# Graph attention on one core: Wh of six graphs computed later from x kept on chip, theta of four graphs spread by TensorE, a fixed order in the first stages

## The chip, the core and the metric

The kernel runs on one core of a Trainium2 chip. TensorE (PE) multiplies, VectorE (DVE) and ScalarE (ACT) work element by element, GpSimd (POOL) does small steps and issues DMAs, SyncE (SP) only issues DMAs. Each engine takes its instructions in order; data pass between engines by semaphores. The metric is the device time of one launch in microseconds (us), the median of several runs.

## What is computed

Two graph-attention layers over 16 graphs (B) of 1024 nodes (N) and 256 features (F). Only layer 0 is touched by the change:

```
Wh  = einsum('bnf,of->bno', h, W)        # h is x
ei, ej = Wh @ a1, Wh @ a2
att = ei[:, :, None] + ej[:, None, :]
att = bn(att, g1, b1)                    # statistics over batch and rows
att = where(att >= 0, att, 0.2 * att)
att = bn(att, g2, b2)
att = softmax(att, axis=2) * adj
h'  = elu(bn(einsum('bij,bjo->bio', att, Wh), g3, b3))
x   = layernorm(x + h')
```

Layer 1 is an attention with four heads over the same adjacency; it takes two more products of x with vectors made from W, w1 and w2 (eight columns, "xw").

## The kernel before

Nodes are tiled as K = 8 blocks of P = 128, features as C = 2 blocks. Layer 0 runs in three stages, each with its own pools of SBUF and PSUM.

**Stage A (lines 224 to 311).** `vectors1` loads W of layer 1 (W1s) and makes the eight extra columns WW on DVE (16 wprod steps). WX holds the transposed W0 (256 columns), W0 times a1 and a2 (2) and WW (8): FX = 266 columns. For each graph, x is loaded (six buffers), two node blocks at a time (kk) are transposed by PE into PSUM (L285), copied by ACT to xT (L291), multiplied with WX by PE (L295) and copied by DVE to wx (L299, three buffers). Columns 0 to 255 go to DRAM (wh_dram, L300), two columns to eT (L301), eight to DRAM (xw_dram, L302). `parameters1` (L196) loads layer 1's small parameters at graph 1 and adds 1 to bias1 at once. `shifted1` (L191) reloads W1s moved by one row; it is called in the attention stage. `casts.behind` makes POOL wait for a datum and then issues a DMA that converts one graph's adjacency from f32 to bf16; it is called at four graphs of stage A, once in the statistics and at every third graph of stage B. `mask` (L139) loads a converted adjacency transposed.

**Stage B (lines 324 to 518).** First the statistics of the first normalisation, a chain of some 40 small DVE steps with two PE column sums (L332) and one POOL power (L148), which ends in ec, c1 and theta. theta and ec are turned to rows by PE (`to_rows`, L341), copied by ACT and stored to DRAM. Then, for each graph, th = theta spread over 128 partitions comes back from DRAM (L435; four buffers, four loads on ACT's queue, the others on SP's), and eight comparisons of th with ec (five on DVE, L440; three on ACT, L444) are multiplied by PE with the powers of ec (L451, 64 products of 7 columns). The sums give the second normalisation's mean and variance (`moments`).

**Attention stage (lines 523 to 653).** `weights` makes e and em for one node block (two ACT and three DVE steps of 128x1024), `aggregate` multiplies em with Wh (L578), `divisors` makes 1/sum (L555, L565), `store` divides (L593) and stores. For one graph the loop runs all k of the first half of the rows, then all k of the second.

Layer 1 (from 821 us on in the profile) follows an order written out by hand (`tc.manual_schedule`). The stages before it are ordered by the scheduler of the language, which places each engine's instructions by its own priorities; calls marked `keep_in_program_order` keep their place.

Of the kernel before, what the change touches and what calls it, by code (L numbers as in the profile page):

```python
# [8 lines left out]
F32 = mybir.dt.float32  # L9
BF16 = mybir.dt.bfloat16  # L10
# [9 lines left out]
P = 128  # L20
# [7 lines left out]
def kernel(  # L28
# [129 lines left out]
    xw_dram = [dpool.tile([N, 2 * H], F32, name=f"xw_dram_{b}") for b in range(B)]  # L158
# [5 lines left out]
    def vectors1(wp, wps):  # L164


        for fc in range(C):
            nc.sync.dma_start(
                W1s[:, fc], W[:, fc * P : (fc + 1) * P, :].rearrange("h p o -> p h o")
            )  # L170
        wbc = wp.tile([P, 2, H, F], F32, name="wbc")
        nc.sync.dma_start(wbc[:, 0], w1.partition_broadcast(P))
        nc.sync.dma_start(wbc[:, 1], w2.partition_broadcast(P))
        for fc in range(C):
            for s in range(2):
                for h in range(H):
                    prod = wp.tile([P, F], F32, tag="prod", name=f"wprod_{fc}_{s}_{h}", bufs=2)
                    nc.vector.tensor_tensor_reduce(
                        out=prod, in0=W1s[:, fc, h, :], in1=wbc[:, s, h, :], scale=1.0, scalar=0.0,
                        op0=ALU.mult, op1=ALU.add, accum_out=WW[:, fc, s * H + h : s * H + h + 1],  # L180
                    )
        pc = wps.tile([P, 2 * H], F32, tag="aps", name="pc")
# [13 lines left out]
    def parameters1():  # L196
        nc.sync.dma_start(bias1, bias.partition_broadcast(P))
        nc.vector.tensor_scalar(bias1, bias1, 1.0, None, ALU.add)
        nc.sync.dma_start(fb_bc[:, 0:H], lb1.partition_broadcast(P))
        nc.sync.dma_start(fb_bc[:, H : 2 * H], lb2.partition_broadcast(P))  # L200
        nc.sync.dma_start(al_bc, alpha.partition_broadcast(P))
        nc.vector.tensor_scalar(om_bc, al_bc, -1.0, 1.0, ALU.mult, ALU.add)
# [3 lines left out]
    with ExitStack() as l0:  # L206
# [17 lines left out]
        with tc.tile_pool(name="apool", bufs=1) as apool, tc.tile_pool(  # L224
            name="aps", bufs=2, space=PSUM
        ) as aps, tc.tile_pool(name="aps_w", bufs=4, space=PSUM) as aps_w:
            vectors1(apool, aps)
            xin = {}

            def load_x(b):  # L230
                xin[b] = apool.tile([P, K, F], F32, tag="x", name=f"x0_{b}", bufs=6)
                nc.sync.dma_start(xin[b], x[b].rearrange("(k p) f -> p k f", p=P))

            rows = apool.tile([P, P], F32, name="rows")
            nc.vector.memset(rows, 0.0)
            w0 = apool.tile([P, C, F], F32, name="w0")
            nc.scalar.dma_start(w0, W0.rearrange("(c p) f -> p c f", p=P))
            at = 0
            col = {}
            for name, v in (  # L240
                ("a1", a1), ("a2", a2), ("g1", g1), ("b1", b1),
                ("g2", g2), ("b2", b2), ("g3", g3), ("b3", b3),
            ):
                n = v.shape[0] // P
                nc.scalar.dma_start(rows[at : at + n, :], v.rearrange("(k p) -> k p", p=P))
                col[name] = (at, at + n)
                at += n
            for b in range(min(6, B)):
                load_x(b)
            pv = aps.tile([P, P], F32, tag="aps", name="pv")  # L250
            nc.tensor.transpose(pv, rows, ident)
            nc.vector.tensor_copy(vecs, pv)

            def vec(name):
                lo, hi = col[name]
                return vecs[:, lo:hi]

            WX = apool.tile([P, C, FX], F32, name="WX")
            nc.vector.tensor_copy(WX[:, :, F2:FX], WW)
            for fc in range(C):  # L260
                pt = aps.tile([P, F], F32, tag="aps", name=f"pw_{fc}")
                for oc in range(C):
                    nc.tensor.transpose(
                        pt[:, oc * P : (oc + 1) * P], w0[:, oc, fc * P : (fc + 1) * P], ident
                    )
                nc.vector.tensor_copy(WX[:, fc, 0:F], pt)
                pa = aps.tile([P, 2], F32, tag="aps", name=f"pa_{fc}")
                for oc in range(C):
                    nc.tensor.matmul(
                        pa,  # L270
                        w0[:, oc, fc * P : (fc + 1) * P],
                        vecs[:, oc : oc + C + 1 : C],
                        start=(oc == 0),
                        stop=(oc == C - 1),
                    )
                nc.vector.tensor_copy(WX[:, fc, F:F2], pa)

            KK = 2
            for b in range(B):
                wx = apool.tile([P, K, FX], F32, tag="wx", name=f"wx_{b}", bufs=3)  # L280
                for kk in range(K // KK):
                    px = aps.tile([P, KK, C, P], F32, tag="px", name=f"px0_{b}_{kk}")
                    for k in range(KK):
                        for fc in range(C):
                            nc.tensor.transpose(  # L285
                                px[:, k, fc, :],
                                xin[b][:, kk * KK + k, fc * P : (fc + 1) * P],
                                ident,
                            )
                    xT = apool.tile([P, KK, C, P], F32, tag="xT", name=f"xT0_{b}_{kk}", bufs=3)  # L290
                    nc.scalar.copy(xT, px)  # L291
                    for k in range(KK):
                        pw = aps_w.tile([P, FX], F32, tag="w", name=f"pw0_{b}_{kk}_{k}")
                        for fc in range(C):
                            nc.tensor.matmul(  # L295
                                pw, xT[:, k, fc, :], WX[:, fc, :],
                                start=(fc == 0), stop=(fc == C - 1),
                            )
                        nc.vector.tensor_copy(wx[:, kk * KK + k, :], pw)  # L299
                nc.sync.dma_start(wh_dram[b], wx[:, :, 0:F])  # L300
                nc.vector.tensor_copy(eT[:, b], wx[:, :, F:F2])  # L301
                nc.sync.dma_start(xw_dram[b].rearrange("(k p) w -> p k w", p=P), wx[:, :, F2:FX])  # L302
                if b % 3 == 1 and b < 12:
                    casts.behind(eT[0:1, b, 0, 0:1])
                if b + 6 < B:
                    load_x(b + 6)
                if b == 1:
                    parameters1()
            while casts.b < 2:
                casts.behind(eT[0:1, B - 1, 0, 0:1])  # L310
            mts = {b: mask(mpool, b, "mt0") for b in range(min(2, B))}

        epool = l0.enter_context(tc.tile_pool(name="epool", bufs=1))
        wh, ebs = {}, {}
# [8 lines left out]

        with tc.tile_pool(name="bpool", bufs=1) as bpool, tc.tile_pool(
            name="bps", bufs=2, space=PSUM
        ) as bps, tc.tile_pool(name="bps_t", bufs=2, space=PSUM) as bps_t:


# [12 lines left out]
            def to_rows(dst, src, nm):  # L341
# [6 lines left out]

            ei = small(qpool, "ei", [B, K])
            nc.vector.tensor_copy(ei, eT[:, :, :, 0])  # L350
            g_mean = column_sums("g_mean", ei)
            e_mean = small(qpool, "e_mean", [1])
# [4 lines left out]
            nc.vector.tensor_scalar(ec, ei, e_mean, None, ALU.subtract)  # L357
            dev_i = small(qpool, "dev_i", [B, K])
            nc.vector.tensor_tensor(
                dev_i, ei, g_mean.unsqueeze(2).to_broadcast([P, B, K]), ALU.subtract  # L360
            )
            nc.vector.tensor_tensor(dev_i, dev_i, dev_i, ALU.mult)
            g_var = column_sums("g_var", dev_i)
            v_mean = small(qpool, "v_mean", [1])
            nc.vector.tensor_reduce(v_mean, g_var, AX.X, ALU.add)
            nc.vector.tensor_scalar(v_mean, v_mean, 1.0 / B, None, ALU.mult)
            ejT = small(qpool, "ejT", [K, B])
            nc.vector.tensor_copy(ejT, eT[:, :, :, 1].rearrange("p b k -> p k b"))
            f_mean = small(qpool, "f_mean", [K])
            nc.vector.tensor_reduce(f_mean, ejT, AX.X, ALU.add)  # L370
            nc.vector.tensor_scalar(f_mean, f_mean, 1.0 / B, None, ALU.mult)
# [8 lines left out]
            nc.vector.tensor_tensor(dev, dev, dev, ALU.mult)  # L380
            var1 = small(qpool, "var1", [K])
            nc.vector.tensor_reduce(var1, dev, AX.X, ALU.add)
            nc.vector.tensor_scalar(var1, var1, 1.0 / B, v_mean, ALU.mult, ALU.add)
            tmp1 = small(qpool, "tmp1", [K])
            inv_std(s1, var1, tmp1)
            nc.vector.tensor_tensor(s1, s1, vec("g1"), ALU.mult)
            s1_b = s1.unsqueeze(2).to_broadcast([P, K, B])
            nc.vector.tensor_tensor(q, q, s1_b, ALU.mult)
            nc.vector.tensor_tensor(
                c1, q, vec("b1").unsqueeze(2).to_broadcast([P, K, B]), ALU.add  # L390
            )

            casts.behind(c1[0:1, 0, 0:1])
            sgn = small(qpool, "sgn", [K])
# [31 lines left out]
            for b in range(B):  # L431
# [24 lines left out]
                if b % 3 == 1:  # L456
                    casts.behind(sums[0:1, 0, 0, b : b + 1])
# [1437 lines left out]
```

## Time and profile before

| | us |
|---|---|
| Timed runs, median of 3 | 2285.81 (2285.52 to 2290.79) |
| The profiled execution's own time | 2298.42 |
| Its span in the trace | 2296.6 |
| PE busy | 2026.6 |
| DVE busy | 1833.9 |
| ACT busy | 1441.7 |
| POOL busy | 938.0 |
| Layer 0, up to the last store's statistics | 821 |

The profile comes from one execution. Busy time is the time in which an engine has an instruction running; matmuls overlap, so a busy PE is not a PE at its peak. "PEclk" or "granted clock" is the TensorE clock that the throttle granted, 1.00 being full speed. A wait is given as the engine and line that waited, the engine and line that ended the wait, the total, the number of times and the longest. SPq and POOLq are DMA issues. A product with f32 operands appears as two passes on PE, so stage A's 256 products are 512 rows.

### The profile page before, as it was taken

How to read it: one execution, taken by the hardware profiler on the slowest of the kernel's cores; microseconds unless marked ns; L12 is line 12 of the kernel's file. 1: busy time of each engine (PE TensorE's matmuls, PEld its weight loads, DVE VectorE, ACT ScalarE, POOL GpSimd, SP SyncE). 2: the span in 40 equal slices, each digit the busy share in tenths (PEclk: the TensorE clock that was granted, in tenths of full speed). 3: DMA queues.
4: the chain of work that ended last, by engine and by line, in shares of the span. 5: the costliest groups of instructions: out<-in, count | busy, mean ns of one | idle time of the engine just before them, and what ended most of it. 6: DMA issues, size and time to landing. Idle time of an engine off the chain costs nothing. (4 is left out here: it accounts for less than half of the span.)

```text
span 2296.6 us, 35722 instructions
## 1 busy us (share of the span) xinstructions
PE 2026.6 (88%) x12023; PEld 1578.7 (69%) x12023; DVE 1833.9 (80%) x4480; ACT 1441.7 (63%) x3156; POOL 938.0 (41%) x1005
## 2 busy tenths in 40 slices
PE   6785368999999955999999999999999999999995
PEld 5574334444444434888788888888888888888885
DVE  3234699999999855889889889789889789789784
ACT  1111677777777523686776776767767767767674
POOL 0000000000000005666666667657667667667671
PEclk9998568999999976999999999999999999999998
DMA  8797969997566126765766666756756756756650
GB/s 243 194 268 179 284 151 202 223 225 193 157 164 165 73 96 192 201 178 172 179 178 173 191 172 171 194 155 167 206 158 166 215 154 168 204 163 173 138 142 21
DMA packets 344669, 404.68 MB, mean 176 GB/s; under 512 B 189929, under 2 KB 291357, under 8 KB 334237
## 3 DMA queue, kind: packets, MB, share of 16 engines
q1 hardware_dynamic: 293533, 258.40, 40.1%
q0 software_dynamic: 49728, 141.39, 25.6%
q10 hardware_dynamic: 1216, 2.51, 0.3%
q8 instruction: 98, 1.61, 0.3%
q14 instruction: 94, 0.77, 0.1%
HBM read 330.90 MB, written 104.88 MB: 190 GB/s over the span
## 5 line engine op out<-in xcount | busy, mean ns | idle before, releaser
L1338 POOL DMA_INDIRECT xc<-xe_dram,ix x640 | 687.3, 1074 | 209.1 <-issue 181.3
L1657 PE MATMUL pv<-W1s,sT 128*128 128x256 f32 x2048 | 503.5, 390 | 0.4 <-ACT sT L1651 0.4
L578 PE MATMUL pa<-em,wh 128*128 128x512 f32 x1024 | 452.0, 599 | 17.7 <-DVE em L542 13.4
L1657 PEld LDWEIGHTS pv<-W1s,sT 128*128 128x128 f32 x2048 | 380.5, 196 | 43.8 <-ACT sT L1651 0.8
L1634 PEld LDWEIGHTS pt<-MX,s 125*128 125x128 f32 x2560 | 350.6, 204 | 30.7 <-ACT sT L1644 9.8
L578 PEld LDWEIGHTS pa<-em,wh 128*128 128x128 f32 x1024 | 193.7, 192 | 251.0 <-issue 235.6
L1634 PE MATMUL pt<-MX,s 125*128 125x100 f32 x2560 | 351.4, 286 | 5.4 <-ACT sT L1644 3.0
L1562 PE MATMUL pu<-xc,w 128*125 128x256 f32 x1280 | 347.1, 391 | 1.3 <-ACT s L1628 1.2
L1628 ACT ACTIVATE s<-pu,z 125x256 f32<-125x256 f32 x640 | 261.5, 474 | 82.8 <-DVE z L1620 57.4
L1671 ACT ACTIVATE m<-v,neg 128x512 f32<-128x512 f32 x256 | 183.7, 718 | 200.2 <-DVE v L1665 142.7
L1562 PEld LDWEIGHTS pu<-xc,w 128*125 128x125 f32 x1280 | 232.6, 192 | 36.5 <-issue 5.7
L1644 ACT COPY sT<-pt 128x500 f32<-128x500 f32 x256 | 144.2, 563 | 110.9 <-PE pt L1634 110.9
L534 ACT ACTIVATE e<-eb,c,s 128x1024 f32<-128x1024 f32 x128 | 155.0, 1236 | 79.0 <-DVE sm L548 42.7
L1714 POOL TENSOR_TENSOR ors<-ors,mhalf 128x1 f32<-128x1 f32 x128 | 110.8, 865 | 202.1 <-DVE ors L1708 200.7
L1665 DVE TENSOR_TENSOR v<-pv,x 128x512 f32<-128x512 f32 x256 | 174.9, 683 | 10.9 <-PE pv L1657 10.5
L538 ACT ACTIVATE e<-e,v,u 128x1024 f32<-128x1024 f32 x128 | 152.3, 1229 | 22.7 <-DVE e L537 16.6
L542 DVE TENSOR_TENSOR em<-e,mt 128x1024 f32<-128x1024 f32 x128 | 155.7, 1218 | 3.4 <-PE pa L578 2.1
L295 PE MATMUL pw<-WX,xT 128*128 128x266 f32 x512 | 130.3, 409 | 27.8 <-DVE wx L299 12.3
L537 DVE SCALAR_TENSOR_TENSOR e<-e 128x1024 f32<-128x1024 f32 x128 | 151.5, 1217 | 0.0
L299 DVE COPY wx<-pw 128x266 f32<-128x266 f32 x128 | 55.0, 434 | 115.6 <-PE pw L295 98.5
L1435 PE MATMUL pz<-IW,h 128*128 128x136 f32 x512 | 90.2, 308 | 56.7 <-DVE fs L1452 33.1
L291 ACT COPY xT<-px 128x512 f32<-128x512 f32 x64 | 34.5, 588 | 165.9 <-PE px L285 165.9
(301 smaller groups left out, 3148.3 us busy)
## 6 DMA issues: line engine op xcount, KB each, us to landing
x<-in_x_dram SPq DMA_DIRECT2D x32, 1024.0 KB
adj<-in_adj_dram POOLq DMA_DIRECT2D x16, 2048.0 KB
rw<-adj SPq DMA_DIRECT2D x32, 1024.0 KB
A<-u_dram SPq DMA_DIRECT2D x128, 250.0 KB
xe_dram<-x SPq DMA_DIRECT2D x16, 1060.0 KB
wh_dram<-wx SPq DMA_DIRECT2D x16, 1024.0 KB
wh<-wh_dram SPq DMA_DIRECT2D x16, 1024.0 KB
h_dram<-hb SPq DMA_DIRECT2D x16, 1024.0 KB
```

The costliest lines, as they stand in the source:

```text
L534: nc.scalar.activation(e, ebs[b], AF.Identity, bias=c1[:, k, b : b + 1], scale=s1[:, k : k + 1])
L537: nc.vector.scalar_tensor_tensor(e, e, SLOPE, e, ALU.mult, ALU.max)
L538: nc.scalar.activation(e, e, AF.Exp, bias=v2[:, k : k + 1], scale=u2[:, k : k + 1])
L542: nc.vector.tensor_tensor(em, e, mts[b][:, k, :], ALU.mult)
L578: nc.tensor.matmul(acc[b, hf, oc].rearrange("p k q -> p q k"), wh[b][:, k, oc * P : (oc + 1) * P], ems[b, k][:, hf * HALF : (hf + 1) * HAL ...
L1338: nc.gpsimd.indirect_dma_start(out=self.xc[:, i, :], out_offset=None, in_=xe_dram[g.b % 2], in_offset=bass.IndirectOffsetOnAxis(ap=g.l.ix[ ...
L1562: nc.tensor.matmul(pu[0:QR, 0:F], c.w[:, k].rearrange("p h q -> p (h q)"), c.xc[:, k, 0:F], start=(i == 0), stop=(i == len(OF[q]) - 1),)
L1628: nc.scalar.mul(f.s[0:QR, i], f.pu[i][0:QR, 0:F], f.z[0:QR, i : i + 1])
L1634: nc.tensor.matmul(self.pt[:, :, :, i], self.first.s[0:QR, i, self.hp * P : (self.hp + 1) * P], MX[0:QR], start=True, stop=True,)
L1657: nc.tensor.matmul(self.pv[:, hh, :], self.first.sT[:, fc, self.hp * HP + hh, :], W1s[:, fc, self.hp * HP + hh, :], start=(fc == 0), stop= ...
L1665: nc.vector.tensor_tensor(self.v2, self.pv, self.g.x[:, self.it].unsqueeze(1).to_broadcast([P, HP, F]), ALU.add)
L1671: nc.scalar.activation(self.m, self.v2, AF.Exp, bias=neg1, scale=1.0)
```

## The change

Stage A and stage B are put under `tc.manual_schedule` for PE, ACT, DVE and SP: the order of the calls is the order of the instructions. POOL, and all that is emitted later, stay with the scheduler.

- Stage A: x is turned two steps (kk) ahead of its product. The first ten graphs are as before, with five x buffers and two wx buffers. For the last six graphs (LATE) only the ten columns 256 to 265 are multiplied (into one PSUM tile, pe); their turned x stays on chip in buffers that the masks (mt) and Wh (wh) use later (`room`). xw is collected in SBUF and stored once. Two casts instead of four. x of graph 0 is loaded first, then W1s and the weight vectors; six small parameter loads go to POOL's queue. bias1 is finished at graph 4.
- Stage B: `Late.make` multiplies the kept x with WX's first 256 columns, one node block (a "late tile") at a time, between the statistics' and the comparisons' products; ACT and DVE copy the results, SP stores them. theta of graphs 0 to 3 is spread by PE transposes and ACT copies (`theta_rows`); graphs 4 to 7 come from DRAM on SP's queue, 8 to 15 on POOL's (eight th buffers). The splits of the powers come after theta. Casts at graphs 1, 6 and 11 only. The masks of graphs 0 and 1 are loaded in stage B.
- Attention: graph 0 runs both halves for each k, and both its stores come after `divisors(0)`; xw is reloaded once as xs1 instead of per graph in layer 1.

In the built program, the scheduler places `shifted1`'s two loads right behind the first five x loads on SP's queue, ahead of the first store of Wh, and the reload xs1 right behind the store of xw. Before, they stood behind the store of graph 3.

```diff
+            def turn(b, kk):
+                px = pxs[b, kk] = aps.tile([P, KK, C, P], F32, tag="px", name=f"px0_{b}_{kk}")
...
+                if b in held:
+                    xT = held[b][:, kk * KK : (kk + 1) * KK]
+                else:
+                    xT = apool.tile([P, KK, C, P], F32, tag="xT", name=f"xT0_{b}_{kk}", bufs=3)
+                xTs[b, kk] = xT
+                nc.scalar.copy(xT, px)
+
+            def product(b, kk):
+                if kk == 0 and b in held:
+                    pes[b] = aps_w.tile([P, K, FX - F], F32, tag="w", name=f"pe_{b}")
+                elif kk == 0:
+                    wxs[b] = apool.tile([P, K, FX], F32, tag="wx", name=f"wx_{b}", bufs=2)
+                for k in range(KK):
+                    n = kk * KK + k
+                    if b in held:
+                        pw, lo = pes[b][:, n], F
+                    else:
+                        pw, lo = aps_w.tile([P, FX], F32, tag="w", name=f"pw0_{b}_{n}"), 0
+                    for fc in range(C):
+                        nc.tensor.matmul(
+                            pw, xTs[b, kk][:, k, fc, :], WX[:, fc, lo:FX],
...
+                    if b not in held:
+                        nc.vector.tensor_copy(wxs[b][:, n, :], pw)
...
+            for n, (b, kk) in enumerate(items):
+                product(b, kk)
+                if kk == K // KK - 1:
+                    finish(b)
+                if n + 2 < len(items):
+                    turn(*items[n + 2])
...
+                def make(self, count, shared):
+
+                    for _ in range(count):
...
+                        pw = bps_w.tile([P, F], F32, tag="w", name=f"pw0_{b}_{k}")
                         for fc in range(C):
                             nc.tensor.matmul(
+                                pw, held[b][:, k, fc, :], WX[:, fc, 0:F],
                                 start=(fc == 0), stop=(fc == C - 1),
                             )
+                        if shared and self.n % 2:
+                            nc.vector.tensor_copy(self.wx[:, k], pw)
+                        else:
+                            nc.scalar.copy(self.wx[:, k], pw)
+                        if k == K - 1:
+                            nc.sync.dma_start(wh_dram[b], self.wx)
...
+            def theta_rows(b):
...
+                        nc.tensor.transpose(
+                            ps[:, k * P : (k + 1) * P],
+                            theta[:, b, hf * KH + k : hf * KH + k + 1].to_broadcast([P, P]), ident,
+                        )
+                    nc.scalar.copy(t[:, hf * HALF : (hf + 1) * HALF], ps)
...
+                if b > 0:
+                    compared(b - 1)
+                if b + 8 < B:
+                    load_th(b + 8, nc.gpsimd)
+                late.make(2 + (b % 2 == 0), True)
+                if b == 3:
+                    mts[0] = mask(mpool, 0, "mt0")
+                if b == 9:
+                    queries(0)
+                    queries(1)
+                    for n in range(min(2, B)):
+                        load(n)
...
-                    hf, k = divmod(n, K)
+                    if b == 0:
+                        k, hf = divmod(n, NH)
+                    else:
+                        hf, k = divmod(n, K)
                     aggregate(b, hf, k)
...
+                if b == 0:
+                    divisors(0)
+                    for hf in range(NH):
+                        store(0, hf)
+                    casts.behind(hb[0][0:1, 0, 0:1])
```

## The prediction

> **What bounds the kernel now.** I read three views in this order: busy time by stretches cut at the stage borders, the waits inside the stages that the change touches, and the timeline around the longest waits. One program runs on one core, so a microsecond taken out of a stage is a microsecond less at the end, unless the next stage waits for something else. The chain of waits that ended last only covers the last microseconds and says nothing about these stages.
>
> The stretches, in order: start; A (the products with W0); the statistics; B (the comparisons); the step to layer 0's attention; its ramp; its steady part; layer 1. Columns: stretch, length, busy time and count for each engine, granted TensorE clock, DMA share, GB/s.
>
> ```profile
> 0.00:21.80 21.80, 5.63 (x28) 5.57 (x28) 10.57 (x89) 2.75 (x4) 2.26 (x9) 1.00 0.95 305
> 21.80:207.20 185.40, 157.16 (x759) 127.88 (x759) 58.40 (x146) 33.30 (x62) 4.22 (x8) 0.94 0.79 209
> 207.20:232.20 25.00, 1.61 (x6) 0.89 (x6) 11.32 (x59) 0.57 (x3) 2.95 (x3) 0.56 1.06 242
> 232.20:308.50 76.30, 35.60 (x1024) 31.39 (x1024) 58.49 (x125) 51.18 (x48) 9.15 (x10) 0.50 1.09 273
> 308.50:320.60 12.10, 0.00 (x0) 0.00 (x0) 8.72 (x29) 5.94 (x6) 1.68 (x1) 0.50 1.13 213
> 320.60:374.60 54.00, 44.15 (x123) 21.78 (x124) 51.91 (x55) 40.14 (x39) 1.09 (x2) 0.82 0.46 110
> 374.60:821.00 446.40, 445.60 (x1288) 216.33 (x1286) 406.83 (x486) 316.08 (x369) 6.04 (x10) 1.00 0.67 169
> 821.00:2296.60 1475.60, 1336.83 (x8800) 1174.86 (x8800) 1227.68 (x3494) 991.76 (x2628) 910.64 (x962) 0.93 0.62 168
> ```
>
> PE fills A (157 of 185 us) and the steady attention; in the statistics, and in B (36 of 76), it stands nearly free while DVE (58 of 76) works and both DVE and ACT wait. The waits of A and B (waiter, releaser: total us, times, longest):
>
> ```profile
> PE pw L295 <- DVE wx L299: 12.3, 1, 12.3
> PE pw L295 <- ACT xT L291: 8.8, 29, 0.6
> PE pw L295 <- DVE om_bc L202: 6.7, 1, 6.7
> ```
>
> ```profile
> ACT d L444 <- DMA th<-th_dram: 31.3, 3, 13.2
> DVE d L440 <- DMA th<-th_dram: 27.8, 3, 11.8
> ```
>
> So A loses 12.3 us to a wx buffer not yet stored, 6.7 to bias1, and a small piece each kk; DVE waits 27.8 us for theta (11.8 before the first comparison, 9.0 and 7.0 later). Why the buffer was late shows on SP's queue:
>
> ```profile
> 73.19 1.26 SPq L193 DMA_DIRECT2D W1s<-in_L_gnn_W_dram  x1
> 77.34 27.30 SPq L232 DMA_DIRECT2D x<-in_x_dram  x1
> ```
>
> ```profile
> 77.00:84.00 7.00, 6.41 (x33) 5.15 (x32) 2.08 (x6) 2.11 (x4) 1.07 (x2) 1.00 0.08 26
> ```
>
> After the shifted load of W1s (127 partitions) was issued, only 0.08 of the DMA engines work at 26 GB/s, and SP is stuck 27.3 us in its next issue.
>
> **Start and A, step by step.** Pitches are from the timeline. A full graph takes 10.06 us: 16 transposes at 0.109 us, 32 passes of 266 columns (an f32 product is two passes) at 0.231, and two waits for xT. The change turns x two kk ahead, so 32*0.231 + 16*0.109 = 9.2 us stay. Ten such graphs: 92, plus 2.5 for slow first passes (the first 16 took 5.83 us against 3.86 later). ACT's 0.59 us copy is covered by two products; uncovered, the 0.86 us per graph come back.
>
> A late graph has 10-column products. The trace has none; the nearest row is pd, 128x1 with a 128x128 f32 weight load, 16 passes in 1.84 us, 0.115 each. Bounds 0.115 and 0.231; I take 0.115, since the weight load is the same and 10 columns are nearer to 1 than to 266. 32*0.115 + 16*0.109 = 5.5 us; six: 33. Upper end: +22 us.
>
> The first product starts at 21.8 now. The changed order loads x of graph 0 first (1 MB), then half of W1s and wbc: 0.5 MB more ahead of the first wprod, about 1.3 us at 380 GB/s, so 10.6. Sixteen wprod (5.7 us), mean and WX (1.3 us after pc now): about 17.8. The six small parameter loads moved to POOL's queue are needed only by graph 1.
>
> bias1's DVE step moves from graph 1 to graph 4: its load (10.7 us of DVE waiting) lies behind three graphs, and the 6.7 us go. If it is not there by then, they come back.
>
> The shifted load stays, and here I expect a new wait. In the built order it stands right behind the first five x, before any store of Wh. [...] At 26 GB/s its 508 KB take 19.5 us. [...] With two wx buffers instead of three, graph 2 can only run 4 us on PSUM buffers (to 43): a stall of 11 to 15 us; I take 14 (bounds 0 and 27).
>
> Later stores: A moves 2 MB per 9.2 us, 217 GB/s, against 340 when no cast runs; two casts instead of four. Cost nothing, at most 3 us.
>
> A then ends at 17.8 + 92 + 2.5 + 33 + 14 = 159 instead of 207.2: **-48**.
>
> **Statistics.** The DVE chain to theta keeps its length (10.2 us): power splits leave it, but pg_var queues behind two late tiles on PE (four passes each, about 0.9 us a tile). Theta now reaches four graphs by 32 transposes and eight ACT copies (0.53 us, row L570): 5 us on ACT, instead of 14.4 us through DRAM. But DVE first does the power splits and the zs moments: eleven at 0.45, four at 0.2, ten at 0.3, about 8.8 us. First comparison 19 us after A instead of 25: **-6**. Graphs 4 to 7 come through DRAM on SP behind the xw store, its reload and one Wh store: about 22 us after theta, needed at 26.
>
> **B.** A graph costs DVE 3.57 us: 16 are 57. To this come 20 DVE copies of late tiles (0.40, row L299): 8; and POOL's interference. Five comparisons take 3.39 us, 3.68 beside a cast's issue, so 0.29 per POOL issue; three casts and eight theta loads: 3.2. [...] Row: the mark copy 0.74 instead of 0.18, the issue 1.15 instead of 0.9. [...] ACT: three activations (3.23) and 1.2 copies (about 0.4) stay below DVE.
>
> PE decides. It has 2.4 late tiles per graph beside 1.86 us of comparison products. Granted clock in B is 0.50 in every row. At 0.50 a pass of 256 columns takes 0.43 us, a tile 1.7: 6.0 us per graph against DVE's 4.3, 27 us more. [...] Nearest row with dense f32 passes paced by DVE: the first 25 us of the attention, clock 0.90. I take open, with 3 us for closed stretches.
>
> B: 57 + 8 + 3 + 3 + 2 (last product) = 73 instead of 76, its 16 us of theta waits included: **-3**.
>
> **After B.** The step shrinks by 1 us (one e is made beside POOL's power). Graph 0's aggregation with both halves per k stays DVE-paced; in the built order its stores come after all weights of graph 1, so PE's graph 1 starts 52 us after the first em; now 54, but with ten products (0.43) already done: **+4** with the cold clock. Steady part and layer 1 have the same instructions; casts reach further into the attention, whose PE row is full with casts and without: 0. Sixteen 32 KB loads leave layer 1, hidden now: 0. mask 1 is issued at B's end, needed 36 us later.
>
> **Sum.** -48 - 6 - 3 - 1 + 4 = **-54**. The profiled execution took 2298.4 us (span 2296.6); its sum is 2244. The three timed runs have a median of 2285.8, 12.6 lower; the same 54 off gives **2232**.
>
> **Rivals.**
> - TensorE's clock stays at 0.50 in B: for it, every row of B; against it, PE would be 93% busy. +27: **2259**; half of it if the clock alternates. Chance 0.19.
> - The shifted load holds SP for its full 27 us and more, the cast on top: A's stall 28 instead of 14: **2246**. Chance 0.15.
> - It goes better: no stall at the start (the cast comes after it) and B at DVE's pace: **2215**. Chance 0.16.
> - Late products cost nearly what full ones do (0.231): +22, **2254**. It would mean that the change removes little PE time from A, and does not do what it says. For it, the first passes at 128x2 took 0.21, on a slow clock. Chance 0.06.
> - Slower: each wx buffer waits for its store, which waits behind an x load on the same queue. Beside a cast SP's queue moved only 1.5 MB in 15 us (100 GB/s): 20 us per graph instead of 9.2, ten graphs +108: **2340**. It decides once A's queue falls below about 140 GB/s throughout; only two casts run there. Chance 0.03.
> - Forecast 0.41.
>
> **Range.** 2206 to 2258: from the better case less 9, for the terms I rounded, to the clock case. What a run of this kernel can tell from no change is about 0.3%, 7 us. Faster 0.96, same 0.01, slower 0.03.
>
> **What would show it.** A ends near 159; one PE wait of 11 to 15 us for wx around 43; no wait for xT or om_bc; late graphs at 5.5 us; first comparison 19 us after A; no th wait in B; clock near 1 in B and 4.4 us per graph. It is wrong if B runs at clock 0.5, if late graphs take 9 us, or if stores stall every graph.

## The result, and the profile after

The changed kernel takes 2276.49 us (median of 20 runs, 2266.22 to 2288.67), the kernel before 2285.66 (20 runs, 2277.93 to 2304.79): ratio 0.995, 95% interval 0.993 to 0.9969. The gain is 9 us, not 54, and the time lies outside the range of 2206 to 2258.

Stretches of the profiled execution after (span 2279.8), cut at the same borders as before; columns as there. A is given in two rows: the ten full graphs, then the six late ones.

```profile
0.00:18.22 18.22, 5.86 (x26) 5.13 (x26) 9.15 (x87) 2.75 (x4) 5.30 (x15) 1.00 0.93 313
18.22:131.90 113.68, 94.75 (x485) 79.80 (x485) 37.53 (x103) 22.94 (x40) 2.17 (x4) 0.92 0.81 235
131.90:185.10 53.20, 52.84 (x279) 52.73 (x278) 2.08 (x15) 13.40 (x23) 0.00 (x0) 0.54 0.19 60
185.10:205.00 19.90, 18.26 (x84) 14.72 (x85) 14.79 (x60) 9.10 (x20) 1.69 (x1) 0.85 0.32 113
205.00:297.80 92.80, 69.76 (x1172) 59.81 (x1170) 64.53 (x146) 55.63 (x67) 8.98 (x14) 0.77 0.99 247
297.80:312.00 14.20, 0.00 (x0) 0.00 (x0) 8.93 (x28) 5.90 (x6) 2.58 (x1) 0.50 0.90 209
312.00:366.00 54.00, 36.49 (x103) 19.59 (x104) 53.77 (x55) 41.28 (x37) 1.10 (x2) 0.78 0.43 108
366.00:820.90 454.90, 454.11 (x1306) 220.55 (x1306) 405.79 (x484) 311.97 (x371) 11.23 (x20) 0.99 0.79 188
820.90:2279.80 1458.90, 1332.95 (x8800) 1172.69 (x8800) 1227.31 (x3494) 991.43 (x2628) 905.49 (x962) 0.93 0.61 170
```

Row three is the six late graphs: 53.2 us, 8.9 each, PE busy for 52.8 of them at a clock of 0.54. Row five is B: 92.8 us instead of 76.3, with DVE busy for 64.5 of them and idle for 28. Layer 0's last product ends at 820.1, before at 820.2: in these two executions the first stages gain 27 us (207.2 + 25.0 against 205.0 at the first comparison), and B (16.5), the step to the attention (2.1) and the attention (8.5) give them back. What is left of the gain in these two profiles lies in layer 1, 1459 us against 1476, where the forecast had put nothing.

The waits that carry this (waiter, releaser: total us, times, longest), for 20 to 70 us and, behind the dots, for B and the step:

```profile
DVE wx L343 <- DMA wh_dram<-wx: 21.1, 1, 21.1
PE pw L338 <- DVE wx L343: 17.6, 1, 17.6
...
ACT wx L430 <- DMA wh_dram<-wx: 24.2, 1, 24.2
DVE wx L428 <- DMA wh_dram<-wx: 22.7, 1, 22.7
PE pw L423 <- DVE wx L428: 14.7, 1, 14.7
ACT e L672 <- DMA wh_dram<-wx: 6.3, 1, 6.3
```

PE waits for xT and om_bc no more, and neither DVE nor ACT waits for theta in B. The two large new waits are for a wx buffer whose store is late, and SP's queue shows why (start, duration, line). The last line is the step: ACT's first e of the attention starts only when the last late store of Wh has landed.

```profile
15.86 3.07 SPq L201 DMA_DIRECT2D W1s<-in_L_gnn_W_dram  x1
19.04 21.08 SPq L202 DMA_DIRECT2D W1s<-in_L_gnn_W_dram  x1
40.21 1.27 SPq L350 DMA_DIRECT2D wh_dram<-wx  x1
...
219.15 45.49 SPq L142 DMA_TRANSPOSE mt<-adj  x1
264.76 0.97 SPq L432 DMA_DIRECT2D wh_dram<-wx  x2
```

Each time one issue holds SP, and the store is next in line. In A it is the issue behind the 127-partition load (L201), for 21 us; in B it is mask 0 itself, for 45 us. And a stretch of full graphs during that load, against a stretch of late graphs:

```profile
30.00:40.00 10.00, 10.00 (x55) 8.54 (x55) 4.34 (x14) 2.93 (x5) 0.50 (x2) 1.00 0.07 26
140.00:160.00 20.00, 20.00 (x100) 20.00 (x99) 0.61 (x4) 5.06 (x9) 0.00 (x0) 0.50 0.15 52
```

In the first row the DMA engines move only 26 GB/s at a share of 0.07 (before: 26 and 0.08), and PE's clock is 1.00. In the second PE is busy for all of the 20 us too, but the clock is 0.50 for all of them.

### The profile page after: what moved, and what is told of

It is laid out like the page before. It is cut to its first block, busy times and chain, and to the rows that moved or that the text cites. A ratio compares the mean times of both kernels' runs of the same rounds, so it can differ in the third digit from the quotient of the medians.

```text
span 2279.8 us, 36099 instructions
## 1 busy us (share of the span) xinstructions
PE 2065.0 (91%) x12248; PEld 1625.0 (71%) x12248; DVE 1823.9 (80%) x4468; ACT 1454.4 (64%) x3192; POOL 938.5 (41%) x1019
## 4 chain that ended last, share of the span: by engine, by line
PE 48%; DVE 19%; issue 17%; DMA 7%; POOL 4%; ACT 4%; SPq 1%; DVEq 0%; ACTq 0%; POOLq 0%
PE pa L716 12%; PE pv L1806 11%; PE pt L1783 8%; PE pu L1711 7%; PE po L1414 3%; POOL xc L1489 3%; DMA x<-in_x_dram 3%; PE pw L338 2%; DMA xc<-xe_dram,ix 2%; DVE d L610 2%; PE pz L1584 2%; DVE v L1814 1%; DVE w L1524 1%; DVE B L1375 1%; DVE w L1520 1%
## 5 line engine op out<-in xcount | busy, mean ns | idle before, releaser
L1820 ACT ACTIVATE m<-v,neg 128x512 f32<-128x512 f32 x256 | 183.7, 718 | 200.4 <-DVE v L1814 145.6
L1863 POOL TENSOR_TENSOR ors<-ors,mhalf 128x1 f32<-128x1 f32 x128 | 113.1, 883 | 207.2 <-DVE ors L1857 205.9
L1584 PEld LDWEIGHTS pz<-IW,h 128*128 128x128 f32 x512 | 77.3, 205 | 77.2 <-issue 44.0
L686 DVE TENSOR_TENSOR sm<-sm,e 128x1024 f32<-128x1024 f32 x96 | 117.4, 1223 | 1.2 <-ACT e L676 1.0
```

The source lines that it names most:

```text
L1584: nc.tensor.matmul(pz[:, oc, :], self.h[:, oc, k * P : (k + 1) * P], IW[:, oc, :], start=True, stop=True,)
L1820: nc.scalar.activation(self.m, self.v2, AF.Exp, bias=neg1, scale=1.0)
```

## The experiments

Theory: three faults took the gain, each with a cure of a few lines: the clock falls under ten-column products; mask 0 holds SP in B; the shifted load holds it in A. Rivals: late products are bound by their weight loads; full DMA engines delay the stores whatever the order; what is gained early is lost later. The runs were on several chips, on which the kernel before took 2286 to 2329 us, so times are given as ratios to runs of before on the same chip (with a 95% interval), and stages by one profiled execution of each run. "Products end" is the end of stage A, "step" the time from the end of B to DVE's first em of the attention, and layer 0 ends with its last product.

**1. The shifted load in two pieces.**

```diff
-        nc.sync.dma_start(W1s[1:P, 0], W[:, 0 : P - 1, :]...)
+        for lo, hi in ((1, 113), (113, P)):
+            nc.sync.dma_start(W1s[lo:hi, 0], W[:, lo - 1 : hi - 1, :]...)
```

> The changed kernel; only the shifted load of W1s is cut: partitions 1 to 112 and 113 to 127 in two DMAs instead of 127 in one. Theory (one engine takes all 127 partitions, SP stands 21 us in its next issue, the store of graph 0 behind it is late, PE waits 17.6 us for a wx buffer): the wait at 44 to 61 us falls below 3 us, products end at 185 - 15 = 170, time 2277 - 15 = about 2261. Rival (the cast of an adjacency and the crowd of loads hold the store, not that one load): the wait stays above 10 us, time 2270 to 2277. Second rival (a gain in the first stage is lost again later): products end at 170, time still about 2277.

```profile
15.99 4.18 SPq L202 DMA_DIRECT2D W1s<-in_L_gnn_W_dram  x2
29.83 0.61 SPq L353 DMA_DIRECT2D wh_dram<-wx  x1
```

Ratio 0.9842 (0.9807 to 0.9876). The two pieces hold SP for 4.2 us, where the whole load and the issue behind it held it for 24 (3.1 and 21.1), and the first store of Wh is issued at 29.8 instead of 40.2. With the edit the scheduler also moved the other shifted load, of the second half of W1s, behind that store. PE's longest wait for a wx buffer falls from 17.6 to 2.8 us, and products end at 164.0. Layer 0 ends at 793.3. The theory holds for the waits and for A's end, and the gain is not lost later. Its "one engine" is an estimate: behind the uncut load the share of the 16 DMA engines was 0.07 (30 to 40 us in the changed kernel), the work of about one. Of the 21 us in A, 5 are another effect: here the clock held for 10 us of late graphs before it fell, against 5.

The same edit in the kernel before:

> The kernel BEFORE the change; only its shifted load of W1s is cut in 112 and 15 partitions. Theory (the slow load cost 12.3 us of waiting for a wx buffer there too): that wait goes, the first stage ends 9 to 13 us earlier (207 to about 196), ratio to before 0.994 to 0.996. Rival (with three wx buffers and four casts another store is late in its place): the stage ends at 203 or later, ratio 0.998 to 1. Its layer 1 is that of before: 1475 if the first two profiles' difference (1476 against 1460) is the chip's scatter, and about 8 to 16 more than the changed kernel's 1487 of the run before, thus 1495 to 1503, if the difference is real.

```profile
71.55 2.38 SPq L194 DMA_DIRECT2D W1s<-in_L_gnn_W_dram  x1
76.12 0.64 SPq L194 DMA_DIRECT2D W1s<-in_L_gnn_W_dram  x1
80.32 0.52 SPq L303 DMA_DIRECT2D wh_dram<-wx  x1
```

Ratio 0.9928 (0.9905 to 0.995): this edit alone in the old kernel is worth about as much as the whole change (0.995 on the first chip, 0.9903 on this one). The store that came 36 us after its predecessor now comes after 10; A ends at 191.3 instead of 207.2, and layer 0 at 804.5. That is 16 us, more than the 9 to 13 that I had expected; a likely reason, not tested, is that the stores and loads behind it come earlier too. Its layer 1 took 1507 us on this chip (see 8).

**2. Late Wh stored on ACT's queue** (`nc.scalar.dma_start(wh_dram[b], self.wx)`), mask 0 left where it is.

> The changed kernel; only the six stores of late Wh go to ACT's queue instead of SP's, where mask 0's transposed load stands in front of one for 45 us. Theory (order on SP's queue): PE's 15 us and ACT's 24 us waits for a wx buffer go, the comparisons take 93 - 22 = about 71 us, time about 2255. Rival (the DMA engines are full there, share 1.1, and any store is late): the waits stay above 12 us, comparisons above 84 us, time above 2268.

Ratio 1.0015 (0.999 to 1.004), a miss. The stores no longer stood behind the mask on SP, but one of them held ACT. ACT's timeline in that run:

```profile
290.54 0.33 ACTq L432 DMA_DIRECT2D wh_dram<-wx  x1
290.92 3.23 ACT L614 ACTIVATE d<-th,ec 128x1024 bf16<-128x1024 f32 x3 [35.18 <-DMA mt<-adj]
```

ACT stood idle for 35.18 us until the mask had landed, and then issued the store. The data have nothing to do with each other, and why ACT waited for it was not shown. The mask itself held SP for 59 us. B took 117 us and the step 29. By its numbers the run is on the rival's side, but with the new wait in it it could not separate the theories; the next one does.

**3. Mask 0 behind the comparisons**, the stores on SP as in the change.

```diff
-                if b == 3:
-                    mts[0] = mask(mpool, 0, "mt0")
...
+            mts[0] = mask(mpool, 0, "mt0")
             mts[1] = mask(mpool, 1, "mt0")
```

> The changed kernel; only mask 0's transposed load is issued after the last comparisons, just ahead of mask 1, instead of beside graph 3. Theory (in the middle of the comparisons it holds SP for 45 us, with the stores of late Wh behind it): no PE wait for a wx buffer above 5 us, comparisons take 70 to 74 us instead of 93; the attention then waits at most 5 us more for its mask, so layer 0 ends 16 to 22 us earlier. Rival (the wait only moves: the mask is late for the attention): comparisons 72, the step to the attention longer by 15 or more, layer 0 ends less than 6 us earlier. Second rival (the casts alone fill the DMA engines): comparisons stay above 85.

Its measure on the same chip, the changed kernel unchanged:

> The changed kernel as it is, on the same chip as the runs beside it, as their measure. Expected as at first: ratio to before 0.995; products end at 185, first comparison 205, comparisons end 298, layer 0 ends at 820. If layer 1 differs from before by 8 us or more again (1460 against 1476 in the first two profiles), that part of the gain is real and was not in the forecast; the rival is that it is scatter between executions.

Ratio 0.9861 (0.9796 to 0.9925) against the changed kernel's 0.9903 (0.9868 to 0.9939): four runs of each do not tell the two apart by time, so the evidence is in the stages. With mask 0 behind B:

```profile
196.60:266.60 70.00, 64.48 (x1172) 56.51 (x1170) 64.83 (x146) 55.79 (x67) 8.99 (x14) 0.95 0.99 283
266.60:285.10 18.50, 0.00 (x0) 0.00 (x0) 8.95 (x28) 5.87 (x6) 2.58 (x1) 0.50 1.18 251
...
ACT e L671 <- DMA wh_dram<-wx: 10.8, 1, 10.8
```

B takes 70.0 us at a clock of 0.95 with the same instructions as above, DMA share 0.99 as there: not the traffic but the order on SP made the 23 us, and PE has no wait for a wx buffer left. The step to the attention grows to 18.5. What it waits for is not the mask but the last late store of Wh: ACT's first e waits 10.8 us for it to land (6.3 in the changed kernel). Whether the two masks, issued right behind that store, slow it down was not tested. Layer 0 ends at 793.1, against 810.8 in the profile beside it: 17.7 us, inside the theory's band.

**4. More columns in the narrow products**: `WIDE = 128` in place of F as the first column, each product in a PSUM tile of its own from which DVE copies the ten columns that are wanted.

```diff
-                        pw, lo = pes[b][:, n], F
+                        pw, lo = aps_w.tile([P, FX - WIDE], F32, tag="w", ...), WIDE
...
+                    if b in held:
+                        nc.vector.tensor_copy(eT[:, b, n], pw[:, F - WIDE : F2 - WIDE])
+                        nc.vector.tensor_copy(xw[:, n, b], pw[:, F2 - WIDE : FX - WIDE])
```

> The changed kernel; only the narrow products of the last six graphs multiply 138 columns of WX instead of 10 (all but the 10 are thrown away), with as many instructions and weight loads. Theory (the granted clock falls to 0.50 since 10-column products leave the array idle although PE counts as busy): the clock stays above 0.9 over these graphs, a graph takes 5.6 to 7 us instead of 8.9, products end 12 to 19 us earlier, time about 2261. Rival (weight loads and their waits make 8.9 us, the clock is a consequence of something else): a graph takes 8.9 us or more and the clock stays 0.50, time 2277 or more.

Ratio 0.9806 (0.9772 to 0.9841). The same 20 us with 138 columns:

```profile
140.00:160.00 20.00, 20.00 (x176) 20.00 (x175) 6.74 (x58) 8.47 (x15) 0.00 (x0) 1.00 0.17 59
```

176 rows instead of 100: nearly fourteen times the columns, and nearly twice as fast. A late graph takes 5.4 us, about the 5.5 of the forecast; products end at 164.6. The weight loads are as many as before, so they are not what made 8.9.

The form of the product had changed with its width, so three more variants, run once each, held the form and changed the width alone (`WIDE = 226`, `F`, `246`):

> As the run with 138 columns in the narrow products, but with 40. If the clock depends on how much of PE's time the array streams columns, 40 columns (the pass stays at 0.116, the time of its weight load) come out between: the clock stays open later than with 10 or flickers, a graph takes 6 to 8 us. If any stream beyond a few columns is enough: 5.4 us as with 138. If 138 was needed: 8.9 us as with 10.

> As the runs with 138 and 40 columns (each narrow product in a PSUM tile of its own, copied at once by DVE), but with 10 columns as in the changed kernel. Theory (the width of the product sets the clock): clock 0.50 again from about 137 us on, a late graph 8 to 9 us, products end at 178 to 186. Rival (the form with its own PSUM tiles and copies kept the clock open): clock 1.00, products end at 160 to 165.

> As the run beside it, with 20 columns. If the border lies between 10 and 20: clock 1.00, products end at about 161. If between 20 and 40: clock 0.50 for most of the late graphs, products end after 175. Anything between (168 to 175): the clock flickers, so there is no sharp border.

| columns | clock, 140 to 160 us | PE rows there | products end |
|---|---|---|---|
| 10, as changed | 0.50 | 100 | 185.1 |
| 10, own tiles | 0.50 | 100 | 183.7 |
| 20 | 1.00 | 190 | 161.9 |
| 40 | 1.00 | 190 | 161.9 |
| 138 | 1.00 | 176 | 164.6 |

The two border cases, first ten columns, then twenty:

```profile
140.00:160.00 20.00, 20.00 (x100) 20.00 (x100) 3.95 (x34) 4.68 (x8) 0.00 (x0) 0.50 0.15 51
```

```profile
140.00:160.00 20.00, 20.00 (x190) 20.00 (x189) 7.22 (x62) 8.91 (x16) 0.00 (x0) 1.00 0.14 48
```

At equal form the width alone decides, and in this stream of products and transposes the border lies between 10 and 20 columns. Ten columns that are thrown away save 22 us. It is not one lucky execution: in all seven profiles with ten-column graphs in a row the clock fell to 0.50 and stayed there until A's end (5.0, 5.3, 6.2 and 6.3 us after the last wide product in four of them, 10.3, 11.5 and 12.7 in the other three), and in the seven with 20 columns or more it stayed at 1.00.

**5. Ten columns, but full graphs in between**: order 0, 1, 2, 10, 3, 11, 4, 12, 5, 13, 6, 14, 7, 15, 8, 9.

> The changed kernel; only the order of graphs in the first stage: 0, 1, 2, 10, 3, 11, 4, 12, 5, 13, 6, 14, 7, 15, 8, 9, so that each narrow graph stands between full ones; narrow products keep 10 columns. Theory (the clock falls only after several microseconds of narrow work on end): the clock stays at 0.9 to 1 up to the end of the stage, products end 14 to 20 us earlier than in the changed kernel (179 to 185), at about 163 to 167. Rival (any narrow graph of 5.5 us is enough to close it): the clock alternates, products end less than 8 us earlier.

```profile
75.00:90.00 15.00, 15.00 (x102) 13.53 (x101) 4.11 (x13) 5.28 (x9) 0.00 (x0) 1.00 0.73 235
90.00:105.00 15.00, 15.00 (x87) 13.55 (x86) 4.24 (x14) 4.10 (x7) 0.00 (x0) 0.80 0.72 234
```

From 65 us to A's end the clock is 1.00 but for one dip to 0.50 of 7 us (99 to 106); products end at 164.5. In A the theory holds without an added column: it is ten-column graphs one behind the other that bring the clock down for good. Ratio 0.9886 (0.9843 to 0.9928): B's wait behind mask 0, left in, was longer here (27.3 us for ACT; B 94.7), and layer 0 ends at 799.6.

**6. The three together** (load in two, 138 columns, mask 0 behind B), then with 20 columns:

> The changed kernel with three edits together: the shifted load cut in 112 and 15 partitions, 138 columns in the narrow products, mask 0 after the comparisons. If the three terms are what the forecast of 54 us lacked and don't overlap: products end at 185 - 21 - 18 = 146 to 150, first comparison 166 to 170, comparisons 72, layer 0 ends 55 to 62 us earlier than in the changed kernel, ratio to before 0.968 to 0.972. Rival (they hide behind one another): layer 0 ends less than 45 us earlier.

> The changed kernel with the three edits, the narrow products 20 columns wide instead of 138. Theory (the three terms explain the miss): products end at 145 to 148, comparisons 68 to 71, step 14 to 18, layer 0 ends at 757 to 762, 58 to 63 us ahead of before (820), ratio to before 0.968 to 0.973. Rival (something else was still missing): layer 0 ends at 766 or later (the forecast's sum has it at 766), ratio above 0.975.

Ratios 0.9715 (0.9688 to 0.9742) and 0.9713 (0.9686 to 0.9741). Stages of the first:

```profile
166.85:236.25 69.40, 65.21 (x1172) 57.06 (x1170) 64.70 (x145) 55.67 (x67) 8.96 (x14) 0.93 0.98 282
236.25:253.56 17.31, 0.00 (x1) 0.00 (x0) 8.95 (x28) 6.75 (x6) 2.58 (x1) 0.54 1.17 250
```

Products end at 149.1 and 148.1, layer 0 at 761.3 and 763.9, 59 and 56 us ahead of the first profile of before, and the version beats both kernels. With the three faults gone the gain in layer 0 is what the forecast had, 54, and a little more. It is not quite the forecast's account: that had priced 14 us of the stall, which the cut load removes too, so without it layer 0 would have ended at 752. The 9 us in between are mostly the step (17.3 against 11; ACT's first e waits 8.4 us for the last late store) and the attention (8 longer than before, against the forecast's 4).

Both runs missed their bands in part. Beside the changed kernel's 810.8 on that chip the first is 49.5 ahead, between theory (55 to 62) and rival (under 45); there the clock had fallen 6 us later than in the first profile of the changed kernel. The second, with 763.9, lies between theory (757 to 762) and rival (766), its ratio inside the theory's band.

**7. Are late products worth it at all?** First with none (LATE = 0), then with none, the load in two and both masks free to go early, then with them held at A's end, then so with two late graphs, and with four and mask 0 early. The last two, and "six, three edits" (the first run of 6), have 138 columns.

> The changed kernel with no late graph at all: all sixteen get the full product in the first stage, none is made beside the comparisons; order, theta by TensorE, buffers and queues stay. Theory (a late graph costs 8.9 us at clock 0.50, as much as a full one at clock 1; and the late products only add the stall behind mask 0 and DVE copies to the comparisons): products end where they do now, 185 (+-4), comparisons take about 65 us instead of 93, time about 2250. Rival (the late products do save first-stage time): products end 15 to 20 us later, comparisons 65, time about 2265 to 2270. Forecast on record: the late graphs save 22 us there, comparisons 62 to 65: about 2270.

> The changed kernel with no late graph, the shifted load cut in two, and both masks issued behind the last products (their buffers are free): everything of the change but the late products, with two of the three faults mended. Products end at about 164 to 166 (against 149 with six late graphs and all three mended), comparisons 62 to 66 (against 69), step 11 (against 17). Theory (late products are worth 16 us in the first stage and cost 4 to 10 behind it): layer 0 ends 4 to 12 us later than with the three edits, ratio to before 0.974 to 0.977. Rival (late products are worth nothing once all is counted): ratio 0.970 to 0.972. Second rival (theta loads wait behind the masks on SP): comparisons 75 or more, ratio above 0.979.

> As the run with no late graph, but both masks are held behind the store of x times W1's vectors, at the end of the first stage. Theory (the six late graphs save 16 us there and cost about as much in the comparisons and the step behind): products end at 164 to 168, comparisons take 58 to 60, the step 12, layer 0 ends within 4 us of the run with three edits (761), ratio to before 0.970 to 0.974. Rival (late products do pay): layer 0 ends at 768 or later, ratio 0.975 or more. Second rival (the masks hold SP in front of theta's loads): a wait for theta above 8 us.

> As the run before, with two late graphs (138 columns in their narrow products), whose x lies in the two Wh buffers; nine of their sixteen tiles fall in the statistics, where DVE and not PE is the limit. Theory (the first late tiles are free, those beside comparisons are not): products end 7 us earlier than with none, comparisons 2 to 3 us longer, layer 0 ends at 755 to 759, ratio to before 0.967 to 0.971: the best. Rival: no better than none or six, ratio 0.971 or more.

> As the run with three edits, but with four late graphs instead of six, so that mask 0 has a buffer of its own and is issued right behind the last products, where the DMA engines are a third busy; no mask in the comparisons. Theory: mask 0 takes about 10 us on SP there and nothing waits for it; products end 2 x 3.5 = 7 us later than with six, comparisons 3 to 5 us shorter, the step to the attention no longer than 12 us: within 4 us of the run with six. Rival (mask 0 holds SP in front of theta's loads and the first late store): comparisons wait over 8 us, slower than with six by 8 or more.

| run | products end | B | step | layer 0 ends | ratio (95%) |
|---|---|---|---|---|---|
| none, rest as changed | 186.2 | 89.1 | 12.3 | 812.2 | 0.9955 (0.9931 to 0.9979) |
| none, load in two, masks free | 189.1 | 59.3 | 12.3 | 784.7 | 0.9811 (0.9776 to 0.9846) |
| none, masks at A's end | 171.2 | 63.6 | 12.3 | 771.1 | 0.971 (0.9689 to 0.973) |
| two, masks at A's end | 160.7 | 66.1 | 12.3 | 764.1 | 0.9703 (0.9679 to 0.9726) |
| four, mask 0 early | 156.1 | 69.6 | 12.3 | 763.1 | 0.9721 (0.9689 to 0.9752) |
| six, three edits | 149.1 | 69.4 | 17.3 | 761.3 | 0.9715 (0.9688 to 0.9742) |

Row one shows that the late graphs as built save little or no time in A (186.2 against 185.1 in the first profile of the changed kernel, 178.9 in the second). Its B missed my 65: DVE waited 16.7 us for a theta that POOL's queue brought 46 us after its issue, beside mask 0. Row two missed too: the scheduler moved the masks up SP's queue, to 62 and 105 us, where they held SP for 10.6 and 7.8 us ahead of a store of Wh; PE waited 17.9 us for wx buffers, and A was 25 us over the expected 164. Row three has neither fault. Against it six late graphs save 22 us in A, give back 11 in B and the step, and end layer 0 10 us earlier, as the rival had it (768 or later without them); but its timed ratio, 0.971, is the theory's. The timed ratios of the last four rows, from two chips, do not tell them apart, so whether late products pay in the end was not settled. Two late graphs, which I had expected to be the best (755 to 759), were not: layer 0 ended at 764.1. The long step goes with six late graphs only: in the other rows ACT's first e waits for no store.

**8. Layer 1.** A load of xw for each graph from DRAM again:

> The changed kernel; only layer 1 loads its 32 KB of x times W1's vectors from DRAM for each graph again, as before, in place of the tile kept on chip. Theory (those sixteen loads cost about half a microsecond each at the start of a graph): time 8 us longer than the changed kernel, ratio to before 0.994. Rival (hidden, as the forecast had it): ratio 0.990 to 0.991 as the changed kernel.

Ratio 0.9914 (0.9886 to 0.9943), not to be told from 0.9903. Open: the ratio of the changed kernel on the second chip means 22 us, its layer 0 was 9.4 ahead there of the first profile of before, and layer 1, from layer 0's last product on, took 1459 to 1507 us in the profiles. The 1507 of the old kernel with the load in two (the longest, near the 1495 to 1503 that I had named for the case that the gain in layer 1 is real) stands beside 1485 to 1503 for kernels with the changed layer 1 on the same chip. Whether a part of the gain lies in layer 1 was not settled.

## Why the prediction was wrong

Its sum had layer 0 end 54 us earlier; in the profile it ended at the same time. Its own sign of being wrong, late graphs of 9 us, came true (8.9). That the kernel came out faster at all was forecast, but in this pair of profiles it does not come from layer 0, so it does not speak for the sum. By its steps:

| step | forecast | measured | off by |
|---|---|---|---|
| first product | 17.8 | 18.2 | 0.4 |
| ten full graphs, cold passes | 94.5 | 96.1 | 1.6 |
| wx stall at the shifted load | 14 (11 to 15) | 17.6 | 3.6 |
| six late graphs | 33 | 53.2 | 20.2 |
| A's end to first comparison | 19 | 19.9 | 0.9 |
| B | 73 | 92.8 | 19.8 |
| step to the attention | 11 | 14.2 | 3.2 |
| attention's ramp and steady part | +4 | +8.5 | 4.5 |

- **The failed term in A** is "a late graph has 10-column products ... I take 0.115". The pitch was right at full clock (47 rows in the first 5.1 us of late work, 0.109 each) and wrong after it: 0.2 at a clock of 0.50 (100 rows in 20 us). The forecast priced a pass by its weight load, and did not ask whether such passes keep the clock up; it asked that of B, where the answer was yes (0.95 in the run with mask 0 moved). Its rival "late products cost nearly what full ones do" had about the right price for this step, +22 (measured +20.2), at a chance of 0.06; and the row that it named, 0.21 for narrow passes on a slow clock, is the pitch that was measured. PE's busy share was no help, being 100% in both states. Why ten columns do not hold the clock is open.
- **The failed term in B** is the one that isn't there. "mask 1 is issued at B's end, needed 36 us later" priced mask 1, and mask 0, moved into B at graph 3, was counted as nothing. It held SP 45.5 us in front of a store of Wh, and B took 92.8 us instead of 73. The run with mask 0 moved shows 70.0, and 69.4 with all three edits. Its choice of an open clock, by a row of 0.90 in the attention of before, was right (0.93 to 0.95 there). Its 3.2 us for eleven issues on POOL's queue, an estimate from the profile of before (0.29 us each), was not measured alone; a B of 70 us, where it had 73, leaves no room for much more.
- **A smaller term of the same kind**: the step was to shrink by 1 us and grew by 2, and by 5 to 7 in the mended runs with six late graphs, since ACT's first e waits for the last late store of Wh. The forecast had no store there.
- **The stall at the shifted load** came at its place (43.6 us against 43) and nearly in its size (17.6 against 14). No run shows what the 14 was made up of; the runs showed 26 GB/s during the load, the next issue held for 21.1 us, the wait of 17.6 us, and 2.8 us with the load in two pieces.
- Right too: the start, 19 us to the first comparison, no theta wait in B, the attention's cold ramp in sign.
- The two failed terms sum to 40 of the 55 us; the stall, the step and the ramp are 11 more. "Slower" stayed out, as forecast: the stores did not stall every graph.

## What to carry to other kernels

A product that is made narrower to save time may no longer keep TensorE's clock up (here 0.50 with ten columns, 1.00 with twenty): read the granted clock of the stretch, not its busy share, and pad the product or mix it with wide ones if it falls. A slow DMA can hold the queue that issues it (here a transposed load for 45 us, and the issue behind a load of 127 partitions for 21), so ask which store or load stands next in that queue, and how many buffers wait on that one. When work is moved beside another stage, list every DMA that moves with it; the one that the forecast did not count was worth 20 us here.

## What the runs showed of the hardware

- Ten columns against twenty: clock 0.50 against 1.00 with PE 100% busy in both (140 to 160 us). The fall came 5 to 6 us after the last wide product in four executions, 10 to 13 in three others.
- The same transposed load held SP 7.5 to 12.7 us in the attention of the changed kernel and 10.4 at B's end; issued well inside B, beside casts on POOL's queue, it held SP 42.6 to 45.5 us in four profiles (the changed kernel; ten columns in own tiles; 20; 40) and 59 in the run with the stores on ACT's queue.
- Behind a load of 127 partitions (26 GB/s, DMA share 0.07) the next issue held SP for 21 us; loads of 112 and of 15 partitions held it for 4.2 us together, and the store behind them was issued in 0.6.
- In the run with the late stores on ACT's queue, ACT stood idle for 35.18 us until a transposed load on SP's queue had landed, and then issued a store that shares no data with it.
